# Re-ordering the opening of a paged-attention kernel, and moving weight and activation loads to other queues

## The chip, the cores and the metric

The kernel runs on one core of one Trainium2 chip. The metric is the device time of one execution in microseconds (us), as the median of several runs of the same program; lower is better.

## The reference, cut to what matters

```python
x = x + einsum('bct,bcd->bdt', x, weights[condition])     # a 32x32 matrix for each of 64 batches
q, k, v = x @ Wq.T, x @ Wk.T, x @ Wv.T                    # 32 query heads, 8 key heads, 128 wide
q, k = rope(rmsnorm(q)*qw, pos), rope(rmsnorm(k)*kw, pos) # pos = cache length + 0..31
k_all = concat([k_cache[block_table], k]); v_all = concat([v_cache[block_table], v])
probs = softmax(where(valid, q @ k_all.T / sqrt(128), -1e30))
x = x + (probs @ v_all) @ Wo.T
```

There are 64 batches of 32 rows, the hidden width is 512, and each batch has 512 cached keys in 16 pages of 32. All numbers are float32.

## The kernel before, in words

**Tiles, steps and slots.** Four batches of 32 rows make a tile of 128 rows, so there are 16 tiles (`NT`). The key heads are done in two passes of four (`NHH`), which gives 32 steps (`Step`); step n does tile n % 16. A step has four batches (`BT`) of four heads (`GH`), which are its 16 slots. In each slot TensorE computes one head's scores (`scores`, L570), the exponential follows on ScalarE (L578), and one slot later come the values (`values`, L628). Into the slots of step n the program puts, piece by piece, the projections of step n+1 (`pieces`, L861: rotation tables, keys, four groups of queries, values), the output projection of step n-1 in slots 8 and 9 (L516), and in slots 13 to 15 the start of step n+2: in the first pass the mix with the conditional matrix (`x1_c`, L357), the transposition to columns (`x1_b`, L365) and the store of the columns to DRAM (L368, started from ScalarE's queue); in the second pass only the load of these columns (`x1_t`, L351, from SP's queue).

**Queries to columns.** A projected group is normed and rotated on VectorE (`norm_rope`, L406 to L437; the power -0.5 is on GpSimd, L418) and lands in one shared tile, `rows`. For step 0 TensorE transposes it (`to_columns`, L445) and ScalarE copies it to `q_cols` and `q_last` (L485). For the other steps VectorE transposes blocks of 32 (L451) and 16 transfers of 80 KB (`spread`, L465, SP's queue) bring `rows` into `q_cols` (batches 0 to 2) and `q_last` (batch 3). Slot 0's scores need batch 0 of them, and the scores against the new keys, `new_scores` (`psn`, L588), need all four batches.

**Orders.** The order on TensorE and on SP, which starts most transfers, is the order of the source (`whole`, L88). Until `opening.close()` (L859) this holds for all engines, except that a planner may put work from later into their streams. After L859 a planner places the instructions of VectorE, ScalarE and GpSimd.

**Completion counters.** In the built program every transfer started from SP or ScalarE carries one of eight completion counters. They are dealt out in turn over both queues together, in the planner's order of time, and a queue does not start a transfer until the one that last had its counter has landed. So a transfer on SP can wait for one that ScalarE has yet to start.

**The opening** (L762 to L859) does step 0's projections, batch 0 and parts of batch 1, with step 1's mix, keys and values between them. `angles` (L133) makes sines and cosines for two tiles at a time; the opening calls it for tiles 0 and 1, and again for 2 and 3.

**Loads.** `Batch` starts the 16 key pages of its batch (`k_t`, L291, 64 KB each) on SP, two batches ahead. `fetch` (L315) gathers cached values into one of three buffers on GpSimd's queue; ScalarE masks them (L328), in order with the exponentials, and a fetch waits for the mask that frees its buffer. The output weights of a pass (`wo`, L249, 16 transfers of 256 KB) go in halves of a group: those of the first pass in slots 4 to 6 of step 0 and 4 and 5 of step 1, those of the second in step 16 from slot 10 and in step 17 up to slot 7, all on SP. An entry such as `(0, 4): (0, 1)` of `output_weights` (L901) means halves 0 and 1 in slot 4 of step 0.

**Buffers named below.** `x1t`, the columns of a tile, has one buffer (`bufs=1`); `ot`, the attention output in columns, also has one, made by `new_ot` (L533) and filled by `turn` (L659), in step 0 from slot 9 on. PSUM tiles tagged `pp` rotate over four buffers.

Of the kernel before, what the change touches and what calls it, by code (L numbers as in the profile page):

```python
# [11 lines left out]
F32 = mybir.dt.float32  # L12
# [7 lines left out]
P = 128  # L20
B, S, HID = 64, 32, 512
# [7 lines left out]
NT = B // BT  # L29
NHH = 2  # L30
GH = HK // NHH
# [24 lines left out]
def cond_resid_paged_attention_kernel(  # L56
# [130 lines left out]
    def steps_of(exact, pools):  # L187
# [46 lines left out]
        def load_w(kind, hh, g=0, part=slice(0, 4), eng=nc.sync):  # L234
            if kind == "q":
                src = wq[:, (hh * QH + g * REP) * D : (hh * QH + (g + 1) * REP) * D]
            elif kind == "o":
                src = wo[(hh * QH + g * REP) * D : (hh * QH + (g + 1) * REP) * D, :]
            else:
                src = (wk if kind == "k" else wv)[:, hh * GH * D : (hh + 1) * GH * D]  # L240
            if part.start == 0:
                wt[kind, hh, g] = wpool.tile(
                    [P, 4, 512], F32, tag=f"w{kind}{g}", name=f"w{kind}{g}_{hh}_{uid}"
                )
            t = wt[kind, hh, g]
            if kind == "o" and not exact:
                src = src.rearrange("(h j p) e -> h p j e", h=REP, p=S)
                for h in range(part.start, part.stop):
                    nc.sync.dma_start(t[h * S : (h + 1) * S, :, :], src[h])  # L249
                return  # L250
            eng.dma_start(t[:, part, :], src.rearrange("(c p) e -> p c e", p=P)[:, part, :])

        def load_parts(which, hh, at):

            if 0 <= at < 2 * len(which):
                load_w(which[at // 2][0], hh, which[at // 2][1], slice(at % 2 * 2, at % 2 * 2 + 2))

        def load_cond_weights(t, eng=nc.sync, kind=mybir.EngineType.SP):
            _, number = nc.values_load_multi_w_load_instructions(
# [76 lines left out]
        class Step:  # L336
            def __init__(self, n):
                self.n, self.hh, self.t = n, n // NT, n % NT
                self.name = f"{n}_{uid}"

        def x1_a(st):

            st.acc = work.tile([P, HID], F32, tag="acc", name=f"acc_{st.name}", bufs=3)
            src = acc_d[st.t] if st.hh else x[st.t * P : (st.t + 1) * P, :]
            nc.sync.dma_start(st.acc, src)

        def x1_t(st):

            if st.hh:
                st.x1t = work.tile([P, KC, P], F32, tag="x1t", name=f"x1t_{st.name}", bufs=1)  # L350
                nc.sync.dma_start(st.x1t.rearrange("p c q -> p (c q)"), x1t_d[st.t])  # L351

        def x1_c(st):
            if st.hh:
# [5 lines left out]
        def x1_b(st):  # L360
            if st.hh:
                return
            pm = ps_p.tile([P, KC, P], F32, tag="pp", name=f"px1t_{st.name}")
            for c in range(KC):
                nc.tensor.transpose(pm[:, c, :], st.acc[:, c * P : (c + 1) * P], ident)  # L365
            st.x1t = work.tile([P, KC, P], F32, tag="x1t", name=f"x1t_{st.name}", bufs=1)
            nc.scalar.copy(st.x1t, pm)
            nc.scalar.dma_start(x1t_d[st.t], st.x1t.rearrange("p c q -> p (c q)"))  # L368

        def rot_tables(st):  # L370

            st.rot = {}
            c, s = cos[:, st.t, :], sin[:, st.t, :]
            for name, w in norm_w.items():
# [119 lines left out]
        def k_b(st):  # L494
            to_columns(st, GH)
# [278 lines left out]
        nc.scalar.dma_start(cond_row, cond.rearrange("(i s) t -> s t i", s=S)[0:1])  # L774
        load_w("k", 0, eng=nc.gpsimd)
        load_w("q", 0, 1, eng=nc.gpsimd)
        batch = Batch(first, 0)
        load_w("q", 0, 2)
        load_w("v", 0)
        x1_a(second)  # L780
        load_w("q", 0, 3)
        later = Batch(first, 1)

# [22 lines left out]
        cached_rows(pages_at, lens_at)  # L806
        nc.vector.memset(vn_bufs[0][:, :, D : D + 1], 1.0)
        nc.vector.memset(vn_bufs[1][:, :, D : D + 1], 1.0)
        trig = work.tile([P, 3, TRIG * HD], F32, tag="w1", name="trig1", bufs=1)
        angles(TRIG, trig)  # L810
        for c in range(RAW):
            fetch(0, c)
        fetch(0, RAW, tag="pn", bufs=1)
        q_a(first, 0)
        k_a(first)
        q_a(first, 1)
        q_b(first, 0)
        head_keys(batch, 0, nc.scalar)
        head_keys(batch, 1, nc.scalar)
        q_a(first, 2)  # L820
        head_keys(batch, 2, nc.scalar)
        head_keys(batch, 3, nc.scalar)
        scores(batch, 0)
        after = Batch(first, 2)
        k_b(first)
        for c in (0, 1):
            batch.fill(c)
            fetch(1, c)
        v_a(first)
        q_b(first, 1)  # L830
        x1_c(second)
        batch.fill(2)
        fetch(1, 2)
        batch.fill(3)
        scores(batch, 1)
        values(batch, 0)
        q_a(first, 3)
        q_b(first, 2)
        x1_b(second)
        scores(batch, 2)  # L840
        head_keys(later, 0, nc.scalar)
        head_keys(later, 1, nc.scalar)
        rot_tables(second)
        k_a(second)
        q_b(first, 3)
        v_a(second)
        scores(batch, 3)
        new_scores(first)
        scores(later, 0)
        new_values(first, 0)  # L850
        values(batch, 1)
        new_values(first, 2)
        for c in range(VC):
            later.fill(c)
# [4 lines left out]
        opening.close()  # L859

        def pieces(st):  # L861
            do = {
                2: (rot_tables,),
                3: (k_a,),
                4: ((q_a, 0),),
                5: ((q_a, 1),),
                6: ((q_a, 2),),
                7: ((q_a, 3),),
                9: ((spread, (0, 1, 3)),),
                11: ((spread, (2,)),),  # L870
                13: (v_a,),
            }
            if st is second:
                do[2] = do[3] = do[13] = ()
            return do

        def count(hh):

# [4 lines left out]
            nc.vector.tensor_reduce(counts[:, hh : hh + 1], good, AX.X, ALU.add)  # L883

        valued, turned = (batch, GH - 1), [batch]
        new_ot(first)
        batch, later = later, after
        unfilled = [(later, c) for c in range(VC)]

        def next_values():  # L890
# [7 lines left out]

        x1_a(steps[2])
        load_cond_weights(2)  # L900
        output_weights = {  # L901
            (0, 4): (0, 1),
            (0, 5): (2, 3),
            (0, 6): (4, 5),
            (1, 4): (6,),
            (1, 5): (7,),
            (NT, 10): (0,),
            (NT + 1, 2): (1,),
            (NT + 1, 4): (2,),
            (NT + 1, 5): (3, 4),  # L910
            (NT + 1, 6): (5, 6),
            (NT + 1, 7): (7,),
        }
        for st in steps:
            ahead = steps[st.n + 1] if st.n + 1 < len(steps) else None
            beyond = steps[st.n + 2] if st.n + 2 < len(steps) else None
# [1 line left out]
            for bt in range(0 if st.n else 1, BT):  # L918
# [5 lines left out]
                for g in range(GH):  # L924
# [14 lines left out]
                    if slot in (8, 9) and st.n:  # L939
                        out_proj(steps[st.n - 1], slice((slot - 8) * QH // 2, (slot - 7) * QH // 2))  # L940
                    if slot == 9:
                        if st.n:
                            new_ot(st)
                        for ba in turned:
                            turn(ba)
                        turned = []
                        if 0 < st.n < NT // TRIG - 1:
                            tmp = work.tile(
                                [P, 3, TRIG * HD], F32, tag="w1", name=f"trig_{st.n}", bufs=1
                            )  # L950
                            with tc.issue_after(last["dve"]), tc.issue_after(last["act"]):
                                angles((st.n + 1) * TRIG, tmp)
# [15 lines left out]
                    for at in output_weights.get((st.n, slot), ()):  # L968
                        load_parts([("o", i) for i in range(GH)], st.hh, at)
# [95 lines left out]
```

## Time and profile before

| What | Value |
|---|---|
| Median of 3 runs (lowest, highest) | 2191.49 us (2189.07, 2192.82) |
| The profiled execution's own time | 2190.95 us |
| Its span, and the mean granted TensorE clock | 2189.2 us, 0.992 |
| TensorE matmuls busy | 2151.3 us, 98% |
| VectorE, ScalarE, GpSimd busy | 55%, 40%, 37% |
| Data moved | 358.77 MB, 164 GB/s |

A line of the timeline gives the start in us, the duration of the merged run of instructions, the engine ("SPq" is SP starting transfers), the source line, the operation, what it writes and reads, the count, and in brackets the idle time before it with what ended that. A line of the waits gives the engine and its waiting instruction, after the arrow what it waited for, then the total, the number of times and the longest.

### The profile page before, as it was taken

The page shows a single profiled execution, that of the slowest core. Times are in us where ns is not written, and L with a number is a line of the kernel's source. Part 1 is how long each engine was busy: PE and PEld are TensorE (multiplying, and loading weights), DVE is VectorE, ACT ScalarE, POOL GpSimd, SP SyncE. Part 2 cuts the span into 40 slices and gives each one's busy share as a digit, 9 for nine tenths or more (in the row PEclk, how much of TensorE's full clock was granted, in tenths as well). Part 3 has the DMA queues.
Part 4 walks back from the last instruction along what each step waited for, and adds up shares of the span by engine and source line. Part 5 has one row for each costly group of instructions (what it writes and reads, how often), then busy time and mean ns, then how long its engine had stood idle before and what let it go on. Part 6 is the DMA issues. An engine that isn't in the chain of part 4 may idle for free.

```text
span 2189.2 us, 41546 instructions
## 1 busy us (share of the span) xinstructions
PE 2151.3 (98%) x12970; PEld 1500.0 (69%) x12970; DVE 1199.7 (55%) x2881; ACT 867.3 (40%) x1574; POOL 806.1 (37%) x1008
## 2 busy tenths in 40 slices
PE   8879999999999999999999999999999999999998
PEld 5657766677766777667777667777667776667775
DVE  5555566655565545556545656445556445656442
ACT  3434444444333443334443334443334443334441
POOL 4433333433343333334333434333334334334330
PEclk9989999999999999999999999999999999999999
DMA  7656555555555555556856865555555655555652
GB/s 227 175 157 176 150 154 145 167 163 159 161 144 158 161 169 154 153 151 189 252 166 173 206 169 160 169 162 163 147 162 160 173 162 155 151 162 161 175 153 62
DMA packets 387863, 358.77 MB, mean 164 GB/s; under 512 B 54737, under 2 KB 316897, under 8 KB 387633
## 3 DMA queue, kind: packets, MB, share of 16 engines
q1 hardware_dynamic: 342912, 215.10, 35.0%
q0 software_dynamic: 41712, 136.66, 21.8%
q10 hardware_dynamic: 3008, 4.25, 0.5%
q8 instruction: 106, 1.74, 0.3%
q14 instruction: 125, 1.02, 0.2%
HBM read 302.59 MB, written 12.58 MB: 144 GB/s over the span
## 4 chain that ended last, share of the span: by engine, by line
PE 97%; DMA 1%; SPq 1%; issue 0%; ACT 0%; DVE 0%; ACTq 0%; DVEq 0%
PE po_x L628 22%; PE ps_x L570 21%; PE pout_x L516 20%; PE pp_q_x L401 20%; PE pp_v_x L401 5%; PE pp_k_x L401 5%; PE pnv_x L612 2%; PE psn_x L588 2%; PE pmix_x L357 1%; SPq L465 0%; DMA wq_x<-in_wq_dram 0%; SPq L291 0%; PE px1t_x L365 0%; DMA x1t_d<-x1t_x 0%; DMA w_sel<-in_w_cond_dram,cond 0%
## 5 line engine op out<-in xcount | busy, mean ns | idle before, releaser
L315 POOL DMA_INDIRECT raw_x<-in_vc_dram,v_row x512 | 539.8, 1054 | 840.3 <-ACT v_x L328 772.5
L578 ACT ACTIVATE pr_x<-ps_x 128x512 f32<-128x512 f32 x512 | 305.8, 597 | 833.8 <-PE ps_x L570 774.1
L628 PEld LDWEIGHTS po_x<-v_x,pr_x 128*128 128x128 f32 x4096 | 517.0, 192 | 125.6 <-issue 115.2
L628 PE MATMUL po_x<-v_x,pr_x 128*128 128x129 f32 x4096 | 552.3, 278 | 1.1 <-issue 1.1
L401 PE MATMUL pp_q_x<-wq_x,x1t_x 128*128 128x512 f32 x1024 | 463.4, 595 | 4.3 <-DMA wq_x<-in_wq_dram 4.3
L516 PE MATMUL pout_x<-wo_x,ot_x 128*128 128x512 f32 x1024 | 450.2, 592 | 0.0
L570 PE MATMUL ps_x<-q_cols_x,kh_x 128*128 128x128 f32 x3072 | 406.9, 275 | 13.1 <-DMA q_cols_x<-rows_x 12.6
L570 PEld LDWEIGHTS ps_x<-q_cols_x,kh_x 128*128 128x128 f32 x3072 | 377.4, 192 | 29.8 <-issue 28.3
L328 ACT ACTIVATE v_x<-raw_x,valid 128x512 f32<-128x512 f32 x512 | 363.0, 716 | 9.5 <-DMA raw_x<-in_vc_dram,v_row 9.5
L516 PEld LDWEIGHTS pout_x<-wo_x,ot_x 128*128 128x128 f32 x1024 | 189.7, 190 | 214.3 <-issue 214.0
L401 PEld LDWEIGHTS pp_q_x<-wq_x,x1t_x 128*128 128x128 f32 x1024 | 186.0, 192 | 190.2 <-issue 185.7
L563 DVE COPY kh_x<-k_t_x 128x512 f32<-128x512 f32 x506 | 206.2, 417 | 195.7 <-PE ps_x L570 159.1
L646 DVE TENSOR_TENSOR nv_x<-po_x,nv_x 128x258 f32<-128x258 f32 x256 | 108.4, 423 | 322.8 <-PE po_x L628 311.0
L418 POOL TENSOR_TENSOR rs_q_x<-ms_q_x,minus_half 128x4 f32<-128x4 f32 x128 | 140.7, 1099 | 176.2 <-DVE ms_q_x L416 176.2
L411 ACT ACTIVATE sq_q_x<-pp_q_x 128x512 f32<-128x512 f32 x128 | 76.6, 598 | 272.9 <-PE pp_q_x L401 171.2
L570 PE MATMUL ps_x<-q_last_x,kh_x 128*128 128x128 f32 x1024 | 135.1, 275 | 0.0
L524 DVE TENSOR_TENSOR acc_x<-pout_x,acc_x 128x512 f32<-128x512 f32 x32 | 22.1, 692 | 199.5 <-PE pout_x L516 199.5
L570 PEld LDWEIGHTS ps_x<-q_last_x,kh_x 128*128 128x128 f32 x1024 | 124.6, 192 | 0.0
L401 PE MATMUL pp_k_x<-wk_x,x1t_x 128*128 128x512 f32 x256 | 116.1, 596 | 0.0
L401 PE MATMUL pp_v_x<-wv_x,x1t_x 128*128 128x512 f32 x256 | 115.2, 592 | 0.0
L415 DVE TENSOR_REDUCE ms_q_x<-sq_q_x 128x4 f32<-128x512 f32 x128 | 86.6, 676 | 49.9 <-ACT sq_q_x L411 48.0
L649 DVE TENSOR_TENSOR o_x<-nv_x,rden 128x256 f32<-128x256 f32 x256 | 108.5, 424 | 6.5
(105 smaller groups left out, 1464.5 us busy)
## 6 DMA issues: line engine op xcount, KB each, us to landing
k_t_x<-in_kt_dram SPq DMA_DIRECT2D x2048, 64.0 KB
q_cols_x<-rows_x SPq DMA_DIRECT2D x372, 80.0 KB
q_last_x<-rows_x SPq DMA_DIRECT2D x124, 80.0 KB
raw_x<-in_vc_dram,v_row POOLq DMA_INDIRECT x512
wo_x<-in_wo_dram SPq DMA_DIRECT2D x32, 256.0 KB
acc_x<-in_x_dram SPq DMA_DIRECT2D x16, 256.0 KB
x1t_d<-x1t_x ACTq DMA_DIRECT2D x16, 256.0 KB
acc_d<-acc_x SPq DMA_DIRECT2D x16, 256.0 KB
```

The source lines that it names most:

```text
L315: nc.gpsimd.indirect_dma_start(out=raw.rearrange("p g d -> p (g d)"), out_offset=None, in_=vc, in_offset=bass.IndirectOffsetOnAxis(ap=v_ro ...
L328: nc.scalar.activation(v_bufs[b % 2][:, c, :, 0:D], raw, AF.Copy, scale=ok)
L401: nc.tensor.matmul(pp, st.x1t[:, c, :], w[:, c, :], start=(c == 0), stop=(c == KC - 1))
L415: nc.vector.tensor_reduce(ms, sq, AX.X, ALU.add)
L418: nc.gpsimd.tensor_tensor(rs, ms, minus_half, ALU.pow)
L516: nc.tensor.matmul(st.po, st.ot[:, i, :], wt["o", st.hh, i // 4][:, i % 4, :], start=(i == 0), stop=(i == QH - 1),)
L563: last["dve"] = nc.vector.tensor_copy(k, ba.k_raw[:, :, g, :]).ins
L570: nc.tensor.matmul(ps[:, c, :], ba.k[g][:, c * P : (c + 1) * P], queries(ba, g), start=True, stop=True,)
L578: last["act"] = nc.scalar.activation(pr, ps, AF.Exp, scale=SCALE).ins
L628: nc.tensor.matmul(ba.po[:, g % 2, :], ba.pr[g][:, c, :], ba.v_t[:, c, g, :], start=(c == 0), stop=(c == VC - 1),)
L646: nc.vector.tensor_tensor(t, ba.po, t, ALU.add)
L649: nc.vector.tensor_tensor(ba.o[:, both, :], t[:, :, 0:D], rd.unsqueeze(2).to_broadcast([P, 2, D]), ALU.mult,)
```

## The change

It has five parts. (1) In the opening, step 1's mix goes ahead of the second group's norm, its transposition behind the first group's, and its key projection ahead of the third group of queries. Its columns lie in the tile of `ot`, and `new_ot` makes that tile for step 0 in slot 9. Its rows come on GpSimd's queue. (2) The sines and cosines of tiles 2 and 3 move down beside the fourth group. (3) Step 1's first group of queries moves into the opening, the other three to slots 4 to 6 of step 0, its values further down; its spread goes out in slot 7 (batches 0 and 3), 10 and 11. (4) Six halves of the first pass's output weights start within the opening and at its end, on SP; those of the second pass go to GpSimd's queue. (5) In the second pass the load of the columns (`x1_t`) goes from SP's queue to ScalarE's.

```diff
-        def x1_a(st):
+        def x1_a(st, eng=nc.sync):
...
-                nc.sync.dma_start(st.x1t.rearrange("p c q -> p (c q)"), x1t_d[st.t])
+                nc.scalar.dma_start(st.x1t.rearrange("p c q -> p (c q)"), x1t_d[st.t])
...
-            st.x1t = work.tile([P, KC, P], F32, tag="x1t", name=f"x1t_{st.name}", bufs=1)
+            if st.n == 1 and not exact:
+                whole = act.tile([P, QH, P], F32, tag="ot", name="x1t_second", bufs=1)
+                st.x1t = whole[:, 0:KC, :]
...
         load_w("q", 0, 1, eng=nc.gpsimd)
+        x1_a(second, nc.gpsimd)
         batch = Batch(first, 0)
...
-        x1_a(second)
...
-        trig = work.tile([P, 3, TRIG * HD], F32, tag="w1", name="trig1", bufs=1)
-        angles(TRIG, trig)
...
-        q_a(first, 1)
+        pp = project(first, wt["q", 0, 1], "pp_q_opening")
+        x1_c(second)
+        finish(first, 1, pp, f"q_{first.name}_1", "q")
         q_b(first, 0)
+        x1_b(second)
         head_keys(batch, 0, nc.scalar)
+        rot_tables(second, ("k",))
+        pp = project(second, wt["k", 0, 0], "pp_k_opening")
+        k_b(first)
+        finish(second, GH, pp, f"k_{second.name}", "k")
...
         scores(batch, 0)
+        for at in (0, 1, 2):
+            load_parts(outputs, 0, at)
         after = Batch(first, 2)
-        k_b(first)
...
+        q_b(first, 1)
         v_a(first)
-        q_b(first, 1)
-        x1_c(second)
...
         values(batch, 0)
+        trig = work.tile([P, 3, TRIG * HD], F32, tag="w1", name="trig1", bufs=1)
+        angles(TRIG, trig)
         q_a(first, 3)
         q_b(first, 2)
-        x1_b(second)
...
-        rot_tables(second)
-        k_a(second)
+        rot_tables(second, ("q",))
+        q_a(second, 0)
         q_b(first, 3)
-        v_a(second)
...
         values(batch, 1)
+        v_a(second)
         new_values(first, 2)
...
+            if st is second:
+                return {
+                    4: ((q_a, 1),),
+                    5: ((q_a, 2),),
+                    6: ((q_a, 3),),
+                    7: ((spread, (0, 3)),),
+                    10: ((spread, (1,)),),
+                    11: ((spread, (2,)),),
+                }
...
-        new_ot(first)
...
+        for at in (3, 4, 5):
+            load_parts(outputs, 0, at)
+        second_outputs = [(0, 10), (0, 13), (0, 15), (1, 1), (1, 3), (1, 4), (1, 5), (1, 6)]
...
                     if slot == 9:
-                        if st.n:
-                            new_ot(st)
+                        new_ot(st)
...
+                    if st.n == 1 and slot in (4, 5):
+                        load_parts(outputs, 0, slot + 2)
+                    if (st.n - NT, slot) in second_outputs:
+                        at = second_outputs.index((st.n - NT, slot))
+                        load_parts(outputs, 1, at, nc.gpsimd)
```

More of the change, by code (lines that the diff above doesn't have):

```diff
@@ L248, in load_w, with load_parts @@
                 for h in range(part.start, part.stop):
-                    nc.sync.dma_start(t[h * S : (h + 1) * S, :, :], src[h])
+                    eng.dma_start(t[h * S : (h + 1) * S, :, :], src[h])
                 return
             eng.dma_start(t[:, part, :], src.rearrange("(c p) e -> p c e", p=P)[:, part, :])
-        def load_parts(which, hh, at):
+        def load_parts(which, hh, at, eng=nc.sync):
             if 0 <= at < 2 * len(which):
-                load_w(which[at // 2][0], hh, which[at // 2][1], slice(at % 2 * 2, at % 2 * 2 + 2))
+                kind, g = which[at // 2]
+                load_w(kind, hh, g, slice(at % 2 * 2, at % 2 * 2 + 2), eng)
+        outputs = [("o", g) for g in range(GH)]
         def load_cond_weights(t, eng=nc.sync, kind=mybir.EngineType.SP):
@@ L339, in __init__ @@
                 self.name = f"{n}_{uid}"
-        def x1_a(st):
+                self.rot = {}
+        def x1_a(st, eng=nc.sync):
             st.acc = work.tile([P, HID], F32, tag="acc", name=f"acc_{st.name}", bufs=3)
             src = acc_d[st.t] if st.hh else x[st.t * P : (st.t + 1) * P, :]
-            nc.sync.dma_start(st.acc, src)
+            eng.dma_start(st.acc, src)
         def x1_t(st):
@@ L365, in x1_b, with rot_tables @@
                 nc.tensor.transpose(pm[:, c, :], st.acc[:, c * P : (c + 1) * P], ident)
-            st.x1t = work.tile([P, KC, P], F32, tag="x1t", name=f"x1t_{st.name}", bufs=1)
+            if st.n == 1 and not exact:
+                whole = act.tile([P, QH, P], F32, tag="ot", name="x1t_second", bufs=1)
+                st.x1t = whole[:, 0:KC, :]
+            else:
+                st.x1t = work.tile([P, KC, P], F32, tag="x1t", name=f"x1t_{st.name}", bufs=1)
             nc.scalar.copy(st.x1t, pm)
             nc.scalar.dma_start(x1t_d[st.t], st.x1t.rearrange("p c q -> p (c q)"))
-        def rot_tables(st):
-            st.rot = {}
+        def rot_tables(st, kinds=("q", "k")):
             c, s = cos[:, st.t, :], sin[:, st.t, :]
-            for name, w in norm_w.items():
+            for name in kinds:
+                w = norm_w[name]
                 cw = work.tile(
@@ L861, in pieces @@
         def pieces(st):
-            do = {
+            if st is second:
[7 more added lines that the diff above has]
+                }
+            return {
                 2: (rot_tables,),
@@ L872, in pieces @@
             }
-            if st is second:
-                do[2] = do[3] = do[13] = ()
-            return do
         def count(hh):
@@ L900, in steps_of @@
         load_cond_weights(2)
[L901 to L913, printed above, removed]
+        for at in (3, 4, 5):
+            load_parts(outputs, 0, at)
+        second_outputs = [(0, 10), (0, 13), (0, 15), (1, 1), (1, 3), (1, 4), (1, 5), (1, 6)]
         for st in steps:
@@ L967, in steps_of @@
                         count(0)
-                    for at in output_weights.get((st.n, slot), ()):
-                        load_parts([("o", i) for i in range(GH)], st.hh, at)
+                    if st.n == 1 and slot in (4, 5):
[3 more added lines that the diff above has]
+                        load_parts(outputs, 1, at, nc.gpsimd)
                     if st.n in (NT - 2, NT - 1):
```

## The prediction

> **What bounds the kernel now.** I read the page first, then TensorE's waits, then the timeline where they lie, then SP's.
>
> From the page, busy times and the chain that ended last:
>
> ```profile
> PE 2151.3 (98%) x12970; PEld 1500.0 (69%) x12970; DVE 1199.7 (55%) x2881; ACT 867.3 (40%) x1574; POOL 806.1 (37%) x1008
> PE 97%; DMA 1%; SPq 1%; issue 0%; ACT 0%; DVE 0%; ACTq 0%; DVEq 0%
> ```
>
> TensorE is the bound. The change takes no matmul away, so all it can win is TensorE's idle time, 2189.2 - 2151.3 = 38 us, and the slow matmuls behind a pause. The waits of TensorE over the whole span say where:
>
> ```profile
> PE ps_x L570 <- DMA q_cols_x<-rows_x: 12.6, 1, 12.6
> PE psn_x L588 <- DMA q_cols_x<-rows_x: 5.3, 1, 5.3
> PE pp_q_x L401 <- DMA wq_x<-in_wq_dram: 4.3, 1, 4.3
> ...
> PE po_x L628 <- issue: 1.1, 1, 1.1
> PE pnv_x L612 <- ACT nv_x L620: 1.0, 1, 1.0
> ```
>
> Each happened once, all before 126 us; from there to the last matmuls TensorE never waits. About 10 us at the very end (the last store) are untouched. So there are two places to win, the opening (4.3 and some ones) and the seam from step 0 to step 1 (12.6 + 5.3). TensorE's timeline shows that seam:
>
> ```profile
> 103.17 1.06 PE L628 MATMUL po_x<-v_x,pr_x 128*128 128x129 f32 x8
> 116.85 2.05 PE L570 MATMUL ps_x<-q_cols_x,kh_x 128*128 128x128 f32 x8 [12.62 <-DMA q_cols_x<-rows_x]
> ```
>
> The queries were in `rows` at 92.2; what was late was their transfer. SP's waits between 98 and 113 us:
>
> ```profile
> SPq L291 <- DMA x1t_d<-x1t_x: 14.7, 1, 14.7
> ```
>
> and its timeline between 104 and 126:
>
> ```profile
> 106.51 5.99 SPq L291 DMA_DIRECT2D k_t_x<-in_kt_dram  x12
> 112.69 5.06 SPq L465 DMA_DIRECT2D q_cols_x<-rows_x  x8
> 117.80 2.49 SPq L465 DMA_DIRECT2D q_last_x<-rows_x  x4
> 120.38 2.43 SPq L465 DMA_DIRECT2D q_cols_x<-rows_x  x4
> ```
>
> SP's fifth key page of batch 4 has the same completion counter as the store of tile 2's columns, which ScalarE starts at 104.10, in slot 15. SP stood 14.7 us until it landed at 106.5, and only then sent 12 pages (0.50 each) and 16 spreads (0.62 each); the last, started at 122.23, landed 2.9 us later, and `psn` ran at 125.25. From landing to `psn`: 18.75 us.
>
> **What the Trainium skill says.** DMA: Bandwidth & Descriptors, "Issuing engines are not separate DMA queues": starting transfers on several engines saves only the time to start them. The trace agrees as to bytes, but here a start is also a wait. The same page, "Anatomy of one DMA — SWDGE (gpsimd) path", puts about 2 us of a transfer into its completion; the column stores took 2.40 and 2.55 us. TensorE: Matmul & The Clock Gate, "Part 1: The HAM clock gate", says that an idle window (about 3.4 us) halves the clock until a busy one has passed. Here it was granted 0.50 from 110 to 125 us, and even the 0.95 us wait at 62 us was followed by matmuls that took some 2.6 us more than warm ones. ScalarE: Activation LUTs, "What ACT_TABLE_LOAD costs", measures 1283 ns; the load at 37.71 took 1.28.
>
> **The change part by part** (against the profiled run's own 2190.95 us).
>
> *Opening.* TensorE stood from 26.4 to 30.64 for the third queries' weights, then ran cold (5.34 us instead of 3.60). The new order has there the mix (0.86), the transposition of step 1's columns (0.45) and its keys (3.44). Their own chain sets them: VectorE's norms follow each other every 3.6 us, so the mix's addition (0.69) comes behind the norm of the keys. That norm ended at 28.6; without `angles` ahead it starts about 1 us earlier, even with 0.8 us more on GpSimd's queue for the moved rows (the 256 KB before the page table; a POOL issue took 0.82). Addition done 28.5, transposition, copy (0.6) at 29.7; but the PSUM tile of the keys is the second group's, free when VectorE has read it, at about 30.8. So step 1's keys run at 30.8, where the third queries ran, cold too, and end at 35.5; the queries, now without wait, at 39.4. Then ScalarE is the tight engine: copy, square (0.6), the norm chain up to the next square (2.9), key copies (0.57), table (1.28), exponential, masks (0.7), and the copy of the second group's columns at about 45.4, 1.4 us after TensorE is ready. Two table loads are added (sines after the second exponential, and back): 2 x 1.28, of which about 0.7 shows at each of the two following column copies. In sum the end of the opening comes at some 67.9, with step 1's first queries done; before, those ended at 70.76. Less 0.6 for slower clock: **-2.3** (bounds +1 and -5, by how much of the pauses and cold matmuls of 1 to 2 us stays).
>
> *Slots 4 to 15*: the same matmuls. The output weights (3 MB) leave the stretch of 73 to 88 us, where the DMA engines were over 0.9 busy, for 40 to 65, where they were under 0.5. The 1.09 us before 98.23 follow a mask that waited 2.02 for its gathered values: **-0.5** (0 to -1.1). `new_ot` in slot 9 costs nothing: the first `turn` was there already, and the last reader of the columns is slot 6.
>
> *The seam.* The wait itself stays: in the changed program the store's counter is that of the tenth page of batch 4. But batches 0 and 3 are spread ahead of it, so behind the landing lie 7 pages x 0.50 = 3.5, 0.2, then 8 spreads, the last one starting 7 x 0.63 = 4.4 later, and 2.9 to land: 11.0 instead of 18.75. Slot 0's scores need the last page (3.2 + 2.2 landing, 0.5 copy), which is earlier. **-7.7** (-6.5 to -8.5). Late next: these eight spreads.
>
> *Second pass, columns on ScalarE's queue.* 16 starts of 0.36 lie behind the copy of the new values, where ScalarE idles 1.26: nothing (uncovered, 6 us in all). They leave SP's queue, but share the counters. For all but two steps the next holder is the eighth page of the same slot's batch: at 1325.5 it would start, the columns land at 1327.3, 1.8 us, against 2.9 us until the copy needs the pages and 4.4 more until TensorE does: nothing. But step 17's load, started in step 15, has the counter of the second transfer of the last spread to step 16. That spread started at 1119.53; the load can start only behind the copy that ends at 1127.1, and lands at 1129.6. Three spreads of 0.62 follow, landing at 1133.8, and `psn` ran at 1131.8: 2.0 us idle, and about 1.5 for a colder clock: **+3.5** (0 to +6). Queued behind on SP are the next 16 pages, then 1.0 us late to their copies, with 3 us in hand.
>
> *Output weights on GpSimd.* 16 starts; POOL's 1 MB loads took 0.82, so 13 us on an engine that is 37% busy. In slots 10 to 16 fetches come every 1.8 us and take 0.95; there a pair of starts makes a fetch late by up to 1 us: **+0.5** (0 to +5). SP is rid of them, which nobody waited for.
>
> Sum: -2.3 - 0.5 - 7.7 + 3.5 + 0.5 = **-6.5**, so 2184.5 against 2190.95; the median stood 0.5 above that run: **2185.0**. About 0.2% (4.4 us) is what a measurement of this kernel can tell from no change.
>
> **Rivals.**
> 1. *No loss in the second pass*: the load lands before the spread matters, or the clock stays up. For it: only 2.0 us are missing. Against: the order on ScalarE is fixed. Then -6.5 - 3.5 = -10.0: 2181.5.
> 2. *The opening gets tighter, not shorter*: the table loads and the norm of step 1's keys push ScalarE's chain, whose idle was 0.2 us at the second scores. If each of the four column copies costs 1.5 us and a cold clock, the opening loses 3 instead of winning 2.3, and -1.2 is left: 2190.3, no change. Against: before, TensorE still had 5.7 us of idle in this stretch to fill.
> 3. *Slower: fetches behind the output weights*. Step 16's slots 10 to 15 leave 1.8 us for each fetch, mask and exponential, in order on ScalarE. At 98.23 a fetch 2.0 us late cost TensorE 1.09. If each of the eight halves does that, 8 x (1.1 + 1.2 cold) = 18.4 us in place of the 0.5 above: -7.0 + 18.4 = +11.4, 2202.9. It decides from 7.0 us lost in all, 0.9 for a half. For it: masks waited 0.16 us for values at 1123.9, so there is little in hand. Against: one fetch has three buffers ahead.
> 4. *The change doesn't do what it says*: the spread for batches 1 and 2 still waits for slot 15. This is in my forecast.
>
> **How the numbers follow.** Forecast 0.58, rival 1 0.17, rival 2 0.15, rival 3 0.10. The forecast's own range is 2181 to 2189. The range of 8 in 10 takes in rivals 1 and 2 with their bounds: 2179 to 2192. Faster by over 0.2% (under 2187.1): rival 1 and most of the forecast, 0.68; slower (over 2195.9): 0.10; within: 0.22.
>
> **What would show it.** In the changed profile: TensorE's longest wait at the seam under 9 us, then one of 4 to 5 at `psn`; SP waiting for `x1t_d` before its tenth page; no wait for `wq`; step 1's keys in the opening near 31; one wait of `psn` of about 2 us near 1125, with SP's spread behind the load of the columns. Wrong would be: the seam's wait gone altogether, several waits of `po` or `ps` between 1175 and 1240, or an opening that ends after 71.

## The result and the profile after

| | Before | Changed |
|---|---|---|
| Median of 20 runs | 2193.3 us (2189.07 to 2200.73) | 2187.55 us (2182.39 to 2193.15) |
| Profiled execution | 2190.95 us, span 2189.2 | 2188.15 us, span 2186.4 |

The ratio of the times is 0.9974, 95% interval 0.9966 to 0.9982: 5.7 us faster, against 6.5 forecast and 2185.0 us predicted. That the total is so close is in part luck: the opening lost where it was to win, and a shorter tail that nobody forecast made up for part of that. The page of the changed kernel, busy times and the chain that ended last:

```profile
PE 2151.0 (98%) x12970; PEld 1497.9 (69%) x12970; DVE 1195.4 (55%) x2881; ACT 869.5 (40%) x1576; POOL 816.6 (37%) x1025
PE 95%; DMA 2%; DVE 1%; ACT 1%; POOL 1%; SPq 0%; issue 0%; DVEq 0%; ACTq 0%
```

TensorE's work is the same to 0.3 us, and it is still the bound. ScalarE has the two added table loads. TensorE's waits, over the whole span:

```profile
PE ps_x L578 <- issue: 9.3, 2, 8.7
PE psn_x L596 <- DMA q_cols_x<-rows_x: 3.8, 2, 2.1
...
PE px1t_x L369 <- DVE acc_x L362: 2.9, 1, 2.9
PE ps_x L578 <- ACT q_cols_x L493: 2.5, 3, 1.2
...
PE ps_x L578 <- DVE kh_x L571: 1.5, 1, 1.5
```

The 12.6 and 5.3 us of the seam and the 4.3 for the third queries' weights are gone. In their place stand 8.7 and 1.8 at the seam, four waits of the opening in the middle rows, and two in the second pass (2.1 of the `psn` row, and the last row). Two of these are labelled "issue": the trace shows no releaser. TensorE's timeline at the seam, with VectorE's copy of the keys just ahead of it:

```profile
114.54 2.05 PE L578 MATMUL ps_x<-q_cols_x,kh_x 128*128 128x128 f32 x8 [8.67 <-issue]
118.94 0.42 PE L596 MATMUL psn_x<-q_cols_x 128*32 128x128 f32 x1 [1.77 <-DMA q_cols_x<-rows_x]
```

```profile
114.02 1.43 DVE L571 COPY kh_x<-k_t_x 128x512 f32<-128x512 f32 x4 [9.24 <-DMA k_t_x<-in_kt_dram]
```

The copy names the cause: the scores wait for the last pages of batch 4. SP's waits and timeline there:

```profile
SPq L473 <- DVE rows_x L459: 16.8, 1, 16.8
SPq L294 <- DMA x1t_d<-x1t_x: 3.9, 1, 3.9
```

```profile
92.70 2.50 SPq L473 DMA_DIRECT2D q_cols_x<-rows_x  x4
95.24 2.50 SPq L473 DMA_DIRECT2D q_last_x<-rows_x  x4
99.21 13.18 SPq L294 DMA_DIRECT2D k_t_x<-in_kt_dram  x16
112.49 4.95 SPq L473 DMA_DIRECT2D q_cols_x<-rows_x  x8
```

SP no longer stands 14.7 us before the fifth page, but it stands 3.9 within the sixteen pages, until the store of tile 2's columns has landed. Eight spreads were sent before the pages and eight come behind. The 16.8 us are SP's wait for the rows of the first eight; the pages of batch 4 stood in the queue behind them. The opening, TensorE's timeline:

```profile
28.87 0.63 PE L369 MATMUL px1t_x<-ident,acc_x 128*128 128x128 f32 x4 [2.86 <-DVE acc_x L362]
30.17 6.75 PE L409 MATMUL pp_k_opening<-wk_x,x1t_second 128*128 128x512 f32 x8 [0.68 <-ACT x1t_second L375]
46.73 1.16 PE L578 MATMUL ps_x<-q_cols_x,kh_x 128*128 128x128 f32 x8 [1.17 <-ACT q_cols_x L493]
```

Step 1's keys fill the old hole and are themselves cold: 6.75 us. In the second pass, TensorE, then SP, then ScalarE:

```profile
1128.83 0.30 PE L596 MATMUL psn_x<-q_cols_x 128*32 128x128 f32 x1 [2.07 <-DMA q_cols_x<-rows_x]
1209.03 1.16 PE L578 MATMUL ps_x<-q_cols_x,kh_x 128*128 128x128 f32 x8 [1.48 <-DVE kh_x L571]
```

```profile
1114.18 11.58 SPq L473 DMA_DIRECT2D q_cols_x<-rows_x  x4
```

```profile
1121.15 0.33 ACTq L355 DMA_DIRECT2D x1t_x<-x1t_d  x1
```

Four spreads that take 2.5 us elsewhere lasted 11.58: behind the first, SP stood 9.3 us for the load of the columns.

### The profile page after: what moved, and what is told of

It is laid out like the page before. It is cut to its first block, busy times and chain, and to the rows that moved or that the text cites. A ratio compares the mean times of both kernels' runs of the same rounds, so it can differ in the third digit from the quotient of the medians.

```text
span 2186.4 us, 41557 instructions
## 1 busy us (share of the span) xinstructions
PE 2151.0 (98%) x12970; PEld 1497.9 (69%) x12970; DVE 1195.4 (55%) x2881; ACT 869.5 (40%) x1576; POOL 816.6 (37%) x1025
## 4 chain that ended last, share of the span: by engine, by line
PE 95%; DMA 2%; DVE 1%; ACT 1%; POOL 1%; SPq 0%; issue 0%; DVEq 0%; ACTq 0%
PE po_x L636 21%; PE ps_x L578 20%; PE pout_x L524 20%; PE pp_q_x L409 19%; PE pp_v_x L409 5%; PE pp_k_x L409 5%; PE pnv_x L620 2%; PE psn_x L596 1%; PE pmix_x L361 1%; DMA x1t_x<-x1t_d 1%; DMA k_t_x<-in_kt_dram 0%; DMA pages_at<-in_pages_v_dram 0%; PE px1t_x L369 0%; PE pp_k_opening L409 0%; POOL raw_x L318 0%
## 5 line engine op out<-in xcount | busy, mean ns | idle before, releaser
L409 PE MATMUL pp_q_x<-wq_x,x1t_x 128*128 128x512 f32 x984 | 442.7, 592 | 0.0
L578 PE MATMUL ps_x<-q_cols_x,kh_x 128*128 128x128 f32 x3072 | 407.8, 276 | 12.6 <-issue 8.7
L409 PEld LDWEIGHTS pp_q_x<-wq_x,x1t_x 128*128 128x128 f32 x984 | 177.6, 190 | 176.5 <-issue 176.5
```

The costliest lines, as they stand in the source:

```text
L409: nc.tensor.matmul(pp, st.x1t[:, c, :], w[:, c, :], start=(c == 0), stop=(c == KC - 1))
L578: nc.tensor.matmul(ps[:, c, :], ba.k[g][:, c * P : (c + 1) * P], queries(ba, g), start=True, stop=True,)
```

## The stages in fourteen profiles

One profile of each kernel is shown; executions differ by some us, mostly in the opening. So the stages are read apart. **Slot 15**: when tile 2's transposition (`px1t`) starts in step 0, the same work being done. **Seam**: from there to the first `psn` of step 2. **Rest**: from there to the first `psn` of step 31; all that differs in it lies in the second pass. **Tail**: from the start of the last store to the end of the span.

| Kernel | Slot 15 | Seam | Rest | Tail | Ratio to before |
|---|---|---|---|---|---|
| before | 102.7 | 91.8 | 1925.6 | 8.5 | |
| b_spread | 102.8 | 92.5 | 1925.3 | 8.2 | 1.0002 |
| b_spread_slot7 | 102.0 | 91.3 | 1926.9 | 8.3 | one time |
| b_store_pool | 98.3 | 79.6 | 1925.6 | 10.7 | 0.9958 |
| b_store_pool_wo_early | 102.9 | 74.8 | 1926.8 | 10.6 | 0.9956 |
| b_best_again (same code) | 104.0 | 75.7 | 1930.6 | 11.3 | 0.9951 |
| changed | 104.4 | 84.6 | 1929.9 | 5.9 | 0.9974 |
| after_again (same code) | 104.4 | 84.1 | 1932.1 | 6.2 | 0.9978 |
| angles_early | 104.1 | 84.2 | 1934.8 | 5.9 | 0.9980 |
| cols_sync | 103.4 | 83.8 | 1927.4 | 7.7 | 0.9990 |
| wo_sync | 100.2 | 83.8 | 1935.2 | 8.6 | 1.0029 |
| wo_as_before | 106.0 | 83.5 | 1933.9 | 8.9 | 1.0009 |
| a_store_pool_cols_sync | 102.2 | 79.1 | 1931.2 | 8.0 | 0.9969 |
| opening_alone | 103.5 | 79.7 | 1927.6 | 10.9 | 0.9964 |

Names with b_ are edits of the kernel before, the others of the changed one. Within the rest, the time from one step's first `psn` to the next is the same in all profiles to within 0.15 us, except from that of step 15 to that of step 19; all differences of the rest arise there.

The experiments were timed in three sets, each on a chip of its own beside the kernel before, whose medians there were 2188.91, 2192.0 and 2193.24 us. So times are compared within a set, and ratios across sets. A ratio on record can differ from the quotient of the two medians beside it by up to 0.0008 (some 2 us), so smaller differences of time decide nothing.

## Experiments on the seam

**b_store_pool**, one edit of the kernel before:

```diff
-            nc.scalar.dma_start(x1t_d[st.t], st.x1t.rearrange("p c q -> p (c q)"))
+            eng = nc.gpsimd if st.n == 2 else nc.scalar
+            eng.dma_start(x1t_d[st.t], st.x1t.rearrange("p c q -> p (c q)"))
```

> The kernel before, with one edit: the store of tile 2's columns (x1t_d, slot 15 of step 0) starts on GpSimd's queue, whose transfers have counters of their own. Theory, shared counters: SyncE's 14.7 us wait before the fifth key page goes; its twelve pages follow at 92 to 98 us, the twelve spreads behind them by 106, landing by 109, and psn of step 1 runs at 109 to 112 us instead of 118.8: 7 to 10 us earlier, and so is all that follows. Rival, bandwidth: the DMA engines (0.9 busy from 95 to 105 us) could not have moved the pages and spreads sooner; then psn comes at most 2 us earlier. Second rival: the store in GpSimd's order holds up the fetches behind it, and a wait of po for gathered values of 1 to 3 us takes the place of part of the gain.

2178.32 us against 2188.91, ratio 0.9958 (0.9945 to 0.9971). SP's timeline:

```profile
81.29 14.04 SPq L291 DMA_DIRECT2D k_t_x<-in_kt_dram  x16
95.52 5.18 SPq L466 DMA_DIRECT2D q_cols_x<-rows_x  x8
100.74 2.70 SPq L466 DMA_DIRECT2D q_last_x<-rows_x  x4
103.53 2.45 SPq L466 DMA_DIRECT2D q_cols_x<-rows_x  x4
```

The pages last 14.04 us instead of 25.53, no wait for the store is left, and the seam falls by 12.2 us, more than expected, with the spreads left in their old slot. TensorE's waits there:

```profile
PE ps_x L571 <- DMA q_cols_x<-rows_x: 2.9, 1, 2.9
PE psn_x L589 <- DMA q_cols_x<-rows_x: 2.7, 2, 2.5
```

So the DMA engines could move the bytes sooner; the start was what waited. The feared wait of `po` for values was 1.6 us, labelled "issue", against 1.1 before. At the seam this one line gains more than the whole change, 12.2 against 7.2 us in single profiles. The ratios, 0.9958 and 0.9974, point the same way, but their intervals overlap, and 4.4 us of this profile's lead lie in the opening, which the edit does not touch.

**b_spread**, the spread's edit alone in the kernel before:

```diff
-                do[2] = do[3] = do[13] = ()
+                do[2] = do[3] = do[13] = do[9] = ()
+                do[8], do[10] = ((spread, (0, 3)),), ((spread, (1,)),)
```

> The kernel before, with one edit: the spreads to step 1 are taken apart, batches 0 and 3 in slot 8 and batch 1 in slot 10 instead of all three in slot 9 (the change has 7 and 10). Nothing else of the change. Theory: the shorter queue behind the store's landing is all of the gain at the seam: SP still stands for the store's counter before the fifth or a later page, but eight spreads fewer follow; from px1t to psn 22.5 us become 14 to 16, and psn of step 1 runs at 111 to 113 us. With no loss in the second pass the kernel ends 3 to 6 us earlier than the changed one. Rival, the early keys and queries of the opening are needed for it: rows are not there in slot 8, the spread waits for them and holds up the pages behind it; then psn comes at 115 us or later.

Ratio 1.0002 (0.9994 to 1.001), seam 92.5: nothing, and the expectation fails. SP's timeline shows why:

```profile
87.41 25.28 SPq L291 DMA_DIRECT2D k_t_x<-in_kt_dram  x16
112.88 2.50 SPq L465 DMA_DIRECT2D q_cols_x<-rows_x  x4
```

In slot 8 the spread still comes behind all pages of batch 4 in SP's order, and the pages still stand 14.9 us.

**b_spread_slot7**, as b_spread, but with `do[7] = ((q_a, 3), (spread, (0, 3)))` in place of slot 8, so that SP has the changed kernel's order from the spread on; but the store's counter falls elsewhere:

> The kernel before with the spread of batches 0 and 3 in slot 7, ahead of the pages of batch 4 on SyncE's queue, and batch 1 in slot 10: SyncE's order from there on is that of the changed kernel. But the output weights stay where they were, and the store's counter is that of the sixth transfer of this spread (q_last). Theory, shared counters: SyncE stands some 10 us within the spread until the store has landed at about 106, and all sixteen pages and eight spreads follow it: psn of step 2 at 193 to 197 us as before (194.5), no gain, though the order is the change's; TensorE's first wait at the seam is for key pages. Rival, the order of spreads and pages alone is the gain: seam of 84 to 85 us from px1t to psn of step 2, as in the changed kernel, instead of 91.8.

```profile
SPq L465 <- DMA x1t_d<-x1t_x: 11.7, 1, 11.7
```

```profile
91.49 2.50 SPq L465 DMA_DIRECT2D q_cols_x<-rows_x  x4
105.66 2.41 SPq L465 DMA_DIRECT2D q_last_x<-rows_x  x4
109.32 8.14 SPq L291 DMA_DIRECT2D k_t_x<-in_kt_dram  x16
117.56 4.95 SPq L465 DMA_DIRECT2D q_cols_x<-rows_x  x8
```

Seam 91.3, no gain, one time of 2192.5 us. The spread itself is stopped, 11.7 us in the middle. The same order on SP goes with 7.8 us won or with nothing, and the trace shows the difference: which transfer has the store's counter. The changed kernel has the early output weights too, and no run takes these alone out of it, so how the 7.8 us divide between order and weights is not shown.

**b_store_pool_wo_early** and, once more, **b_best_again**: b_store_pool and the twelve first transfers of output weights where the change has them (six ahead of the pages of batch 2, six ahead of those of batch 3).

> The kernel before with two edits: the store of tile 2's columns on GpSimd's queue, and the first twelve output weight transfers where the change has them, six within the opening and six behind it, instead of between the pages of batches 3 and 4. Theory: SyncE then sends the pages of batch 4 some 8 to 10 us earlier, the spreads start when their rows and buffers are there (about 92 us), and the waits left at the seam with the first edit alone (2.9 us before ps, 2.5 before psn) go; seam from px1t to psn of step 2 74 to 76 us instead of 79.6, about 4 us faster than the first edit alone and the fastest kernel of all. Rival: the spread of batches 0, 1 and 3 waits in slot 9 for the readers of its buffers, so starting earlier wins nothing: 79 us. Second rival: the transfers within the opening delay its key pages and columns, and the opening loses 1 to 3 us.

> The same kernel as b_store_pool_wo_early, once more, beside the other runs of this chip: the store of tile 2's columns on GpSimd's queue and the first output weights early, all else as before. Seam 74 to 76 us again; 9 to 12 us faster than the kernel before.

2180.95 us against 2192.0, ratio 0.9956 (0.9942 to 0.9969); again 2183.39 against 2193.24, 0.9951 (0.9934 to 0.9968). Seams of 74.8 and 75.7, as expected: the early weights are worth 4 to 5 us there. TensorE's timeline in the first of them:

```profile
108.69 0.41 PE L589 MATMUL psn_x<-q_cols_x 128*32 128x128 f32 x2 [3.11 <-DMA q_cols_x<-rows_x]
```

The scores wait for nothing any more; the last spreads remain. The times don't show these 4 us: the ratio is that of b_store_pool within the intervals, with an opening that came 4.5 us later in the first profile.

## Experiments on the second pass

**cols_sync**: `x1_t` starts its load with `nc.sync.dma_start` again.

> The changed kernel, with the second pass's loads of x1t_d back on SyncE's queue (part 5 undone). Theory, shared counters: the load for step 17 no longer holds the counter of the second transfer of the last spread to step 16, so TensorE's wait of 2.07 us before psn at 1128.8 goes; psn of steps 17 and later come 2.5 us earlier than in the changed kernel. The wait of 1.48 us for kh_x at 1209 goes too if the late columns (SP stood 6.8 us for them) delayed the key pages: then 4.3 us in all. Rival, bytes: the wait for kh_x comes from the seven output weight transfers (1.8 MB in 22 us, DMA engines 0.97 busy), then it stays and 2.5 us is all. Second rival, the two waits have nothing to do with the queue of the load: no difference, 0.

The 2.07 us at 1128 are gone, as the counters say. Rest 1927.4, 2.6 us less than the changed kernel. TensorE does not wait for `kh_x` any more either, but this decides nothing about its cause, because a new wait stands just ahead of it and gives the pages as much time:

```profile
1201.82 3.67 PE L409 MATMUL pp_k_x<-wk_x,x1t_x 128*128 128x512 f32 x8 [1.43 <-DMA x1t_x<-x1t_d]
```

On SP's queue the columns can be late for step 18's keys. Seven of the nine profiles with the columns on SP have waits with this label, 0.45 to 4.3 us in sum; none of the five with ScalarE's queue has one. The time, 2187.81 against 2188.91 us, ratio 0.999 (0.9983 to 0.9997), does not show the 2.6 us. The tail took back 1.9, and by the ratios (0.9974 and 0.9978 for the changed kernel, on other chips) undoing this part won nothing and may have lost some 3 us.

**wo_sync**: the second pass's output weights on SP's queue, in the change's slots (`load_parts(outputs, 1, at)`).

> The changed kernel, with the second pass's output weights back on SyncE's queue, in the slots in which the change puts them (only the queue of part 4 undone). Theory, shared counters: two more SyncE starts per slot shift the counters, so that the columns for step 19, loaded in step 17, hold the counter of a transfer in the middle of a spread to step 18: a new wait of psn of 1 to 2.5 us near 1261, besides the one at 1128.8, which stays at 2.1. Theory, bytes in 1185 to 1210: the same bytes are asked for in the same slots, so the 1.48 us wait for kh_x stays. Rival, GpSimd's queue itself (starts of 0.6 us ahead of fetches): the wait for kh_x goes, and the whole is 1.5 to 2 us faster than the changed kernel.

Ratio 1.0029 (1.0018 to 1.0039), 4.6 us slower than before. TensorE and SP between 1240 and 1290 us:

```profile
PE psn_x L596 <- DMA q_cols_x<-rows_x: 2.3, 1, 2.3
```

```profile
SPq L473 <- DMA x1t_x<-x1t_d: 7.7, 1, 7.7
```

The forecast wait is there, at 1262. It came from counting transfers alone. TensorE waited 3.0 us for `kh_x` as well, in a later slot (1226.5 us), so such a wait does not need GpSimd's queue.

**wo_as_before**: the weights in the queue and the slots of before:

```diff
+        second_outputs = {(0, 10): (0,), (1, 2): (1,), (1, 4): (2,), (1, 5): (3, 4), (1, 6): (5, 6), (1, 7): (7,)}
```

> The changed kernel with the second pass's output weights back in the slots and on the queue of before (part 4's second half undone), columns still on ScalarE's queue. Theory, bytes: the wait for kh_x near 1209 (1.5 and 1.9 us in two profiles of the changed kernel) came from seven weight transfers within 22 us beside the key pages, so it goes or falls under 0.5. Theory, counters: the number of SyncE's transfers between columns is again odd for the spread, as with wo_sync: psn waits 2.1 to 2.7 us near 1128 and once more, 2 to 2.5 us, near 1262. From psn of step 2 to that of step 31: 1929.5 to 1931 us, against 1929.9 and 1932.1. Rival: the wait for kh_x came from the columns alone and stays at 1.5 or more.

Ratio 1.0009 (1.0 to 1.0017). No wait for `kh_x` is left, although SP stood 3.9 us for the columns before these pages: it came from the early weights. From 1185 to 1210 us the DMA engines were 0.97 busy in the changed kernel, with seven weight transfers beside 27 pages. `psn` waited 1.8 us at 1128 and 4.2 near 1262 (more than expected), and the rest took 1933.9, 3 us over the expectation. With the weights on SP, in this run and in wo_sync, the ratio is 0.35 and 0.55% above that of the changed kernel. Part of it lies in the tail, which is 3.1 and 2.7 us longer.

**a_store_pool_cols_sync**: cols_sync and the store on GpSimd's queue.

> The changed kernel with two edits: the second pass's column loads on SyncE's queue, and the store of tile 2's columns on GpSimd's queue. Theory, shared counters: SyncE no longer stands for the store (3.9 us in the changed kernel), so the last eight spreads leave about 4 us earlier and the seam from px1t to psn of step 2 takes 80 to 81 us instead of 84.6 (it can't fall as far as in the kernel before with that edit, 79.6, because the spread of batches 0 and 3 waits for its rows ahead of the sixteen pages). With 2.6 us from the columns, some 6 to 7 us faster than the changed kernel on the same chip. Rival: the pages, not the spreads, are what the scores of slot 0 wait for, and they are as late as before; then the seam stays at 83 to 84.5.

Seam 79.1, slightly better than expected: SP still waits 14.7 us for the rows ahead of the pages. But the columns came 3.46 us late to step 18's keys, so the rest is no better than the changed kernel's. 2184.21 against 2192.0 us, ratio 0.9969 (0.9959 to 0.998).

## Experiments on the opening

**after_again**, the changed kernel without an edit:

> The changed kernel once more, unaltered, for a second profile of its opening and a time on the chip of the runs beside it. Three profiles of the changed opening so far reached the transposition of tile 2's columns (slot 15 of step 0, the same work done) at 104.4, 103.4 and 100.2 us, three of the opening of before at 102.7, 98.3 and 102.8. Theory, the opening gains and loses by the run and not by the order: between 100 and 104.5 here; the waits at 1128 (2.1 us, psn) and 1209 (1.5 us, kh_x) are there again, within 0.6 us, since the order of the queues fixes them. Rival, those waits are chance: one of them is missing.

2186.61 against 2192.0, ratio 0.9978 (0.9968 to 0.9987). Slot 15 at 104.4, `psn` at 1128 waits 2.7 us, `kh_x` 1.9: the waits come with the order. What they cost does not: the clock granted to TensorE was at 0.50 for 3.4 us behind this wait for `kh_x`, and the step took 3.7 us longer than before, against 1.8 in the changed kernel's first profile.

**angles_early**: `angles(TRIG, trig)` ahead of the first `fetch` again.

> The changed kernel with the second table of angles back in its old place, at the head of the opening (part 2 undone, without the two added loads of ScalarE's table). My prediction's step: VectorE's addition for step 1's mix, which ended at 27.5 to 28.9 us in five profiles, comes 1 us later (28.5 to 30), with the transposition waiting as much longer and more often on a cold clock; the two loads of 1.28 us save 1.4 us at the column copies later (TensorE's three waits for q_cols copies, 2.5 us in sum, become 1 or less). Together 0 to 1 us later at slot 15's transposition (100 to 105 us). Rival, the table loads are the dearer part: 2 to 3 us earlier there, 98 to 101.5 us, and the whole 2 us faster than the changed kernel. From then on all as in the changed kernel.

2190.32 against 2193.24, ratio 0.998 (0.9972 to 0.9988), as the changed kernel. The mix's addition ends at 30.2, 1.5 us later than in the changed kernel; slot 15 comes at 104.1, within the scatter. But TensorE's waits for column copies stayed:

```profile
PE ps_x L578 <- ACT q_cols_x L493: 2.5, 3, 1.2
```

Without the two table loads these 2.5 us are the same, so the loads are not their cause. The rest of 1934.8 is a third price of the wait for `kh_x`: 3.5 us in this profile, then 6.8 us at a clock of 0.50, 6.7 us in all.

**opening_alone**: the changed opening on b_store_pool_wo_early, all else as before:

> What the change's opening is worth on the best seam: the changed kernel with everything behind the opening as in the kernel before (columns on SyncE's queue, spread of batches 0, 1 and 3 in slot 9, output weights of the second pass in their old slots and queue) and the store of tile 2's columns on GpSimd's queue. So it is b_store_pool_wo_early with the changed opening. Theory from five profiles of each opening (tile 2's transposition at 98.3 to 102.9 us before, 100.2 to 104.4 changed): the order wins nothing, the transposition comes at 100 to 104.5, the seam takes 74 to 76.5 us, the second pass from psn of step 2 to psn of step 31 1925 to 1927 us, and the time is within 3 us of b_store_pool_wo_early. Rival, the predicted gain of the opening is real and was hidden by the seam: then 2 to 3 us faster than b_store_pool_wo_early.

2185.83 us beside 2183.39 of b_best_again: no gain. The seam took 79.7, not 74 to 76.5. The changed opening costs there: SP stood 14.1 us for one of VectorE's key copies ahead of pages of batch 4, against 4.6 in b_best_again, so the spreads left 4.3 us later (99.59 and 95.31). Why that copy came later was not followed further.

## Why the prediction was right, and where not

| Step | Forecast | Measured |
|---|---|---|
| Opening and slots 4 to 15 | -2.8 | +2.0 (mean of 7 profiles against 4) |
| Seam | -7.7 | -7.8 (mean of 6 profiles: 84.0 against 91.8) |
| Second pass, both parts | +4.0 | +4.3 in the pair of profiles; +5.4 by means of 3 (+4.3 to +9.2) against 7 |
| Tail | 0 | -2.4 (means of 3 against 3) |

**Seam: right, by its mechanism.** That the wait stays in a smaller form, that the store's counter is that of the tenth page, and that fewer spreads follow were all seen. From the start of the tenth page (108.95, when the store had landed) to `psn` took 10.0 us for the 11.0 of the working. Only the split was off: `psn` waited 1.8 us behind the scores and not 4 to 5. (The 2 us of completion that the prediction takes from the skill stand on that page for transfers started from GpSimd. The forecast did not need them: the store, started from ScalarE, landed 2.40 us after its start in the kernel before and 2.54 in the changed one.) Rival 4 was, as said, part of the forecast; b_spread_slot7 shows how near the other outcome was.

**Opening: wrong.** Means of seven changed openings (those with the change's code up to slot 15) and of the four of before: 103.4 and 101.5, each scattering by 2 us, so a gain of 2.8 is not there, and a loss of 2 is likely but not certain. The prediction's own sign of being wrong, an opening that ends after 71, came true. The step that failed is "In sum the end of the opening comes at some 67.9"; it came at 71.26. Up to the addition (28.72) and the start of the keys (30.17 for 30.8) it was right. Then the keys took 6.75 instead of the 4.7 of the working (30.8 to 35.5; the third queries, as cold, had taken 5.34), the three column copies cost 2.46 instead of 1.4, and the values of step 1 waited 0.95 for ScalarE. These three terms and the earlier start make up the 3.4 us. Rival 2 had named a tighter opening, but its reason, the table loads, fell with angles_early. The gain of 0.5 in slots 4 to 15 did not come either: `po` waited 1.13 us again for gathered values, at 100.5.

**Second pass: right in sum, partly by luck.** Rival 1, no loss, is out. The 2.07 us at 1128 were forecast as 2.0. The 1.5 for a cold clock did not come (1.00 was granted from 1110 to 1140 us; the wait cost 2.53 to the next step). In its place came the wait for `kh_x`, 1.79 to the next step here, 3.7 and 6.7 in the two other profiles of this second pass. The sentence "0.5 (0 to +5)" for the output weights had put their price into starts on GpSimd's queue, and the bytes beside the key pages were not counted; with the weights back in their old slots (wo_as_before) the wait is gone. Rival 3, fetches behind those starts, was not seen. Unforecast as well: on ScalarE's queue the columns were late in none of five profiles, on SP's in seven of nine.

**Tail: not foreseen.** "About 10 us at the very end (the last store) are untouched" failed. From the start of the last store to the end took 8.2 to 8.5 us in three profiles of before's program with or without the spread's edit, 5.9 to 6.2 in three with the change, and 10.6 to 11.3 in the four that have before's second pass and the store on GpSimd. It goes with the program and not with the run, and the traces show what ends last. It is part 4 that counts. GpSimd's closing instruction (a DRAIN, which the views above leave out) took 8.3 to 8.5 us in all nine profiles whose second pass has its output weights on SP's queue, and 1.05 to 1.13 in the five that have them on GpSimd's. In the first group the other engines wait at the end for this DRAIN (in the kernel before it ends 7.64 us behind the start of the last store); in the second, SP's closing waits come last (5.0 to 5.3 us behind that start in the three with the change, 6.9 and 7.2 in the two others). wo_sync, which differs from the changed kernel by the queue of these weights alone, has the long DRAIN (8.40) and a tail of 8.6. In the four with 10.6 to 11.3, another instruction of GpSimd's, of 2.2 us, runs before it. Why the DRAIN is short or long is not shown.

So the pair of profiles differs by 2.8 us: -7.2 in the seam, +4.3 in the second pass, +1.6 up to slot 15, +1.0 in the last step, -2.6 in the tail. The medians differ by 5.7 because the profiled execution of before was 2.35 us faster than its median, and that of the changed kernel 0.6 slower. What the other executions of before lost is in no trace.

## What to carry over

When a queue stands at a transfer that depends on nothing, ask which transfer had its completion counter last, and count transfers: at the seam, moving one store off the shared counters won more than re-ordering the spreads. Moving a load between queues re-deals every later counter, so look for new collisions in all steps, and count its bytes beside what is moving then. Read a gain by stages from several profiles before you credit it to an edit: here an opening that lost and a tail that nobody aimed at nearly cancelled.

## What the runs showed of the hardware

The Trainium skill, DMA: Bandwidth & Descriptors, "Issuing engines are not separate DMA queues", lets one expect only the time of starting from a choice of queue. Here one 256 KB store moved from ScalarE's to GpSimd's queue shortened the seam by 12.2 us, through the counters; the bytes were the same.

The clock granted to TensorE was 1.00 or 0.50 in all fourteen profiles, never between, and the stretches at 0.50 lasted 3.41 us or a multiple of it (only the last of a run is cut by the end). So the price of a pause in the opening goes by steps. Step 1's keys, eight matmuls, took 3.70 us in the two profiles with no such stretch there (after pauses of 0.53 and 0.54 us), 5.33 to 5.40 in the three with one (1.80 to 2.45), and 6.21 to 6.75 in the three with two (2.86 to 3.24), each with a second pause of 0.7. In the old order, the third queries took 3.67 us after 2.14, with no stretch, but 5.37 after 2.74, with one.

The skill's TensorE: Matmul & The Clock Gate, "Part 1: The HAM clock gate", speaks of an idle window of about 3.4 us; here 1.8 and 0.7 us were enough to pay for. The length of a pause alone does not decide: in after_again 2.73 us at 1128 were followed by no stretch at 0.50, and 1.85 us at 1209 by one. The scatter of the opening follows this in part: the earliest slot 15 of each order (98.3 and 100.2 us) belong to profiles whose clock stayed up, but a_store_pool_cols_sync, whose clock stayed up there too, came at 102.2.
